# A second MoE call with rows cleared ahead, roots on ScalarE, and the pieces of attention's last eleven steps dealt out anew

## Chip, cores and metric

The kernel runs on one core of one Trainium2 chip. The metric is device time of the whole launch in microseconds, median of several executions.

## What is computed

Six residual updates on 2048 tokens of 128 channels (8 sequences of 256), in fp32. Cut to what matters here:

```python
x = x + 0.5 * moe(layernorm(x))          # first expert stage, f = 0
x = x + attention(layernorm(x))          # 16 heads of 8 channels
x = x + 0.5 * moe(layernorm(x))          # second expert stage, f = 1, same weights
x = x + 0.5 * channel_mix(layernorm(x))
x = x + gated_conv(layernorm(x))
x = x + 0.5 * channel_mix(layernorm(x))

def moe(s):
    h = rmsnorm(s @ W_in.T) * in_norm_w
    logits = h @ Wr.T
    idx = top2(logits + expert_bias)
    gates = softmax(logits[idx])                       # over the two
    out = sum over the two experts e of gates[e] * rmsnorm((silu(h @ Wg[e].T) * (h @ Wu[e].T)) @ Wd[e].T)
    return rmsnorm(out) @ W_out.T
```

`x` is not layer-normed on its own ahead of `W_in`: the kernel folds the mean into the weight and divides by one root of (mean square + scaled variance), called `ri` below.

## The kernel before

**Tokens.** `x` stays on the chip in four chunks of 512 tokens (four tiles of 128). PE, DVE, ACT and SP execute instructions in the order in which the code emits them; whatever is emitted first stands first in each engine's queue. GpSimd (POOL) keeps the order of the powers and scatters too.

**An expert stage** has three parts. `dispatch` (one call for each block of tokens: five blocks of 2 or 4 tiles, `LATE` being 4, 4, 4, 2, 2 for f = 1) has pieces: `turned` (transposes `pxt_f`, copied to `xnt_f`), `product` halves (`pin_f`, copied to `u_f`, squares summed into `ss_f`), `measured` (variance into `z_f`), `normed` (`ri_f`: for f = 0 a Sqrt on ACT and a reciprocal on DVE, for f = 1 a power on POOL), `logits` (`lg_f`), `scaled` (rows `hrow` on ACT), two `choices` (top 1 and top 2, six to eight small DVE operations each), `places` (ranks `prank_f` by matmuls, then `at_row`, `posi`: the row of each token in a table of rows sorted by expert), and `rows` (two indirect scatters for each tile, from POOL, into `hs` in DRAM).

`hs` has a region of 2304 rows of 129 floats for each of eight experts. `table` counts tokens for each expert and works out 24 turns (15 of 256 rows, 9 of 128). `zeros` writes 256 zero rows behind each expert's last row, four DMAs from SP and four from ACT, each with a start row from the count. `experts` then fetches for each turn the weights of its expert (`w_f`, 832 KB) and its rows (`hst_f`), three turns ahead, and runs gate (`pg_f`), up (`pu_f`), down (`py_f`) and a scatter of results into `y`. `combine` fetches `y`, weighs, norms, multiplies with `W_out` and adds to `x`.

**Attention** is a loop of 32 steps `s` (8 sequences times 4 groups of heads) and three to drain, each with halves a and b. TensorE makes the scores twice, once to find the largest (`pm`, DVE reduces it to `m`, transposed in `pmt`, added to the query rows as `qa`) and once transposed (`ps`), ACT takes the exponent (`es`), and two steps later `po` averages the values. `ps` has a single pair of banks, so `ps` of a half step waits until `es` of the one before has read it. Everything else is cut into pieces hung on a half step by `at(s, half, ...)`: the end of the first expert stage for chunks 1 to 3 (`combine`'s pieces), the norm and the query, key and value rows of each next chunk (`norm_sums` to `values`), the output of each sequence (`turn_back`, `turn_heads`, `out_heads`: `pot`, `rc`, `cc`, `pcc`, `ct`, `pwo`, added to `x`), and the pieces of the second dispatch (`leaving[0]` to `leaving[4]`). Most of these take their PSUM tile from one bank with the tag `sa`.

`to_heads` brings queries and keys into lanes of 32 partitions by a DRAM round trip: `heads` out, then four loads `qk` from SP. The first step to use chunk n's lanes is 8n.

The last sequence's output can be made only after step 31's average, that is after `osb` of half step (33, b). From there the code emits, in (34, a), the output of the last sequence, the end of block 3, and the whole of block 4. Then `table`, the gates and the experts follow.

## Time and profile before

| | |
|---|---|
| three runs | 680.30, 681.46, 682.06 us |
| profiled execution | 660.66 us in all, span 658.9, TensorE clock 0.92 |
| busy share | PE 79%, DVE 55%, ACT 42%, POOL 30% |
| first expert turns | about 66 to 185 us |
| attention's scores | from 204 us; `osb` of the last sequence at 396.87 us |
| second stage, first gate | 433.54 us; last down product ends about 546 us |
| tail | to 658.9 us |
| DMA | 69.80 MB; HBM written 14.38 MB |

Times of pieces are microseconds from the start of the span of the profiled execution. "Idle before <- X" names what ended an engine's idle time. In section 2 of the page a digit is the busy share of a slice of 16.5 us in tenths. The profiled execution is some 21 us shorter than the median of the runs, so a sum made on it is carried over as a difference.

### The profile page before, as it was taken

To read this page: it belongs to the slowest core of one execution; us is meant where nothing else is said; L and a number is where in the kernel's file an instruction comes from. 1 tells how busy PE (TensorE), PEld (TensorE's weight loads), DVE (VectorE), ACT (ScalarE), POOL (GpSimd) and SP (SyncE) were. 2 spreads that over 40 slices of the span, in tenths; PEclk is the share of its full clock that TensorE was granted. 3 is DMA by queue.
4 is the path that set the end of the run, shared out by engine and by line. 5 is a ranking of instruction groups with operands and counts; after the bars stand their busy time and mean duration, and the time that the engine had idled before them with its cause. 6 is when DMAs were issued, how large, how long until landed. Compare 5 with 4: busy or idle time off the path is not lost. (4 is left out here: it accounts for less than half of the span.)

```text
span 658.9 us, 11485 instructions
## 1 busy us (share of the span) xinstructions
PE 520.4 (79%) x3945; PEld 412.0 (63%) x3945; DVE 360.7 (55%) x1120; ACT 275.0 (42%) x677; POOL 197.9 (30%) x206
## 2 busy tenths in 40 slices
PE   4530999999948988898898984179989992579996
PEld 3530899999935545555554652169979991458885
DVE  4664346544433566765866664724434441667676
ACT  3450233223332465565654662113223230867355
POOL 0476067523331100102004516303333333521110
PEclk9999999999965899999999996579999997779999
DMA  6016577777521302021030101466776774100002
GB/s 212 33 48 171 183 210 242 213 226 216 171 81 32 65 34 33 1 52 14 1 66 22 37 10 41 105 219 197 234 212 205 217 219 115 31 0 2 1 1 64
DMA packets 39753, 69.80 MB, mean 106 GB/s; under 512 B 4939, under 2 KB 30066, under 8 KB 39568
## 3 DMA queue, kind: packets, MB, share of 16 engines
q1 hardware_dynamic: 34000, 59.55, 31.6%
q0 software_dynamic: 4544, 8.47, 3.8%
q10 hardware_dynamic: 1152, 1.06, 0.6%
q8 instruction: 31, 0.51, 0.3%
q14 instruction: 26, 0.21, 0.1%
HBM read 55.60 MB, written 14.38 MB: 106 GB/s over the span
## 5 line engine op out<-in xcount | busy, mean ns | idle before, releaser
L617 POOL DMA_INDIRECT y<-yrow_f,idx_f x78 | 76.6, 982 | 140.8 <-ACT sg_f L583 79.7
L955 ACT ACTIVATE es<-ps 128x1024 f32<-128x1024 f32 x64 | 65.4, 1022 | 59.0 <-PE ps L918 36.0
L428 POOL DMA_INDIRECT hs<-hrow,posi_f x64 | 62.0, 968 | 87.5 <-DVE ri_f L355 35.5
L938 DVE TENSOR_REDUCE m<-pm 128x4 f32<-128x1024 f32 x64 | 77.5, 1220 | 18.1 <-PE pm L901 18.1
L918 PE MATMUL ps<-qa,qk 32*128 32x256 f32 x512 | 75.4, 408 | 14.6 <-ACT es L955 10.3
L901 PE MATMUL pm<-qk 32*128 32x256 f32 x512 | 80.7, 419 | 5.1 <-DMA qk<-heads 3.7
L574 PE MATMUL pg_f<-ht_f,w_f 128*128 128x256 f32 (+1 forms) x384 | 79.6, 352 | 2.6 <-DVE idx_f L615 1.4
L597 PE MATMUL py_f<-w_f,hg_f 128*128 128x128 f32 x624 | 78.2, 276 | 2.6 <-DVE yrow_f L608 2.6
L597 PEld LDWEIGHTS py_f<-w_f,hg_f 128*128 128x128 f32 x624 | 75.2, 192 | 4.8 <-DVE yrow_f L608 3.4
L574 PE MATMUL pu_f<-ht_f,w_f 128*128 128x256 f32 (+1 forms) x384 | 76.5, 343 | 0.0
L590 DVE TENSOR_TENSOR hg_f<-pu_f,sg_f 128x1024 f32<-128x1024 f32 (+1 forms) x48 | 49.2, 1025 | 46.8 <-PE pu_f L574 46.7
L583 ACT ACTIVATE sg_f<-pg_f 128x1024 f32<-128x1024 f32 (+1 forms) x48 | 41.5, 864 | 67.1 <-PE pg_f L574 67.1
L574 PEld LDWEIGHTS pg_f<-ht_f,w_f 128*128 128x128 f32 x384 | 63.1, 197 | 9.1 <-DVE idx_f L615 1.6
L607 ACT ACTIVATE ysq_f<-py_f 128x128 f32<-128x128 f32 x78 | 21.1, 274 | 109.2 <-PE py_f L597 98.1
L574 PEld LDWEIGHTS pu_f<-ht_f,w_f 128*128 128x128 f32 x384 | 61.5, 193 | 6.0
L918 PEld LDWEIGHTS ps<-qa,qk 32*128 32x128 f32 x512 | 44.0, 187 | 31.8 <-ACT es L955 21.6
L901 PEld LDWEIGHTS pm<-qk 32*128 32x128 f32 x512 | 47.8, 193 | 10.2 <-DMA qk<-heads 6.2
L608 DVE TENSOR_TENSOR yrow_f<-py_f,w_f 128x256 f32<-128x256 f32 (+1 forms) x48 | 18.0, 375 | 52.1 <-ACT ysq_f L607 52.1
L566 DVE TENSOR_SCALAR ht_f<-pht_f,pack 128x256 f32<-128x256 f32 (+1 forms) x48 | 20.7, 432 | 41.8 <-PE pht_f L564 41.7
L564 PE MATMUL pht_f<-ident,hst_f 128*128 128x128 f32 x78 | 17.5, 290 | 31.6 <-DMA hst_f<-hs 31.6
L965 PE MATMUL po<-es,v 128*32 128x256 f32 x512 | 35.1, 393 | 0.0
L152 POOL TENSOR_TENSOR cf_f<-cf_f,mhalf 128x8 f32<-128x8 f32 (+1 forms) x9 | 13.5, 1504 | 67.4 <-DVE cf_f L673 65.9
(257 smaller groups left out, 822.8 us busy)
## 6 DMA issues: line engine op xcount, KB each, us to landing
w_f<-in_wall_dram SPq DMA_DIRECT2D x48, 832.0 KB
hst_f<-hs SPq DMA_DIRECT2D x30, 129.0 KB
y_f<-y SPq DMA_DIRECT2D x14, 258.0 KB
pack<-in_pack_dram SPq DMA_DIRECT2D x1, 1729.0 KB
heads<-qkc SPq DMA_DIRECT2D x3, 512.0 KB
qk<-heads SPq DMA_DIRECT2D x12, 128.0 KB
y<-yrow_f,idx_f POOLq DMA_INDIRECT x78, 5.0
hst_f<-hs SPq DMA_DIRECT2D x18, 64.5 KB
```

The costliest lines, as they stand in the source:

```text
L428: ins = nc.gpsimd.indirect_dma_start(out=hs, out_offset=bass.IndirectOffsetOnAxis(ap=st["posi"][:, t, k : k + 1], axis=0), in_=hrow[:, t, ...
L574: nc.tensor.matmul(ph[:, k, :], w[t][:, o + k * P : o + k * P + P], ht[t], start=True, stop=True)
L583: nc.scalar.activation(sg, pg, AF.Silu)
L590: nc.vector.tensor_mul(hg[t], pu, sg)
L597: nc.tensor.matmul(py[:, s, :], hg[t][:, k, ts(s, P)], w[t][:, 2 * DFF + k * D : 2 * DFF + k * D + D], start=(k == 0), stop=(k == NFC - 1),)
L607: nc.scalar.activation(sq[:, s], py[:, s], AF.Square, accum_out=yrow[:, s, D : D + 1])
L617: ins = nc.gpsimd.indirect_dma_start(out=y2, out_offset=bass.IndirectOffsetOnAxis(ap=idx[:, s : s + 1], axis=0), in_=yrow[:, s, :], in_off ...
L901: nc.tensor.matmul(sc[:, jj, i, :], qs[c][r, g, col + i * P : col + (i + 1) * P], ks[c][r, g, col : col + S], start=True, stop=True,)
L918: nc.tensor.matmul(sc[:, jj, i, :], ks[c][r, g, col + i * P : col + (i + 1) * P], tops[s][r, :], start=True, stop=True,)
L938: nc.vector.tensor_reduce(m, sc, AX.X, ALU.max, negate=True)
L955: nc.scalar.activation(es, sc, AF.Exp, scale=scale)
L965: nc.tensor.matmul(po[32 * j : 32 * j + 32, :], vs[c][:, (b % 2) * 2 + i, (g % 2) * (H // 2) + (g // 2) * 4 + j, :], ess[s, j // 2][:, j % ...
```

## The change

- There are two row tables in DRAM, one for each expert stage. The first is zeroed as before. For the second, `zeros` isn't called; `clear_rows` writes zeros over all its 18432 rows, in 12 DMAs of 1536 rows from ACT, hung on attention's half steps (s, b) for s = 2, 3, 4, 8 to 12 and 16 to 19. `first` is worked out for f = 0 only.
- The last two blocks of the second dispatch take `ri` as Sqrt on ACT and reciprocal on DVE. `root_table` (one Sqrt on a scalar tile, which loads the table of that function) is emitted in (33, b), ahead of `normed` of block 3. In the first stage the copy of the token numbers comes ahead of the root.
- For f = 1 the first three turns fetch rows ahead of weights, and the first turn's weights come in three DMAs: gate, up, and down with the norm weights.
- Query and key rows of chunks 1 to 3 are made half a step earlier each; for chunk 1 the norm is earlier too.
- The pieces of blocks 0 to 4 of the second dispatch are hung anew, most of all from step 20 to the end. In (34, a), block 3's choices and rows and block 4's pieces are dealt out between the pieces of the last sequence's output.

In the built program TensorE, DVE and POOL have the same work as before but for the powers (two fewer on POOL) and, on DVE, two reciprocals more and `first` once less; ACT has two roots, one scalar root, two table loads and 12 DMAs more and four DMAs fewer; SP has four zero DMAs fewer and two weight DMAs more.

```diff
-    hs = tc.dram_tile([HS_ROWS, ROW], F32, name="hs")
+    hss = [tc.dram_tile([HS_ROWS, ROW], F32, name=f"hs{f}") for f in range(2)]
...
             if f == 0:
+                nc.vector.tensor_copy(hrow[:, :, :, D].bitcast(I32), tokid[:, slots])
+            if f == 0 or i >= len(parts) - 2:
                 nc.scalar.activation(ri, ri, AF.Sqrt)
                 nc.vector.reciprocal(ri, ri)
-                nc.vector.tensor_copy(hrow[:, :, :, D].bitcast(I32), tokid[:, slots])
             else:
                 power_of(ri, ri, mhalf.to_broadcast([P, nt]))
...
-        first = t_([P, E], "first", I32)
-        nc.vector.tensor_tensor(first, pc, base, ALU.add)
-        zeros(f, first)
+        if f == 0:
+            first = t_([P, E], "first", I32)
+            nc.vector.tensor_tensor(first, pc, base, ALU.add)
+            zeros(first)
...
+    def clear_rows(i, n):
+        m = E * REGION // n
+        dst = hss[1][1 + i * m : 1 + (i + 1) * m, :].rearrange("(p r) w -> p r w", p=P)
+        nc.scalar.dma_start(dst, zero[:, 0:ROW].unsqueeze(1).to_broadcast([P, m // P, ROW]))
...
-            nc.sync.dma_start(w[t], a["wall"][bass.ds(e, 1), :, :].rearrange("o p f -> p (o f)"))
+            wall = a["wall"][bass.ds(e, 1), :, :].rearrange("o p f -> p (o f)")
+            ends = (0, DFF, 2 * DFF, WALL) if f and t == TURNS[0] else (0, WALL)
+            for o, end in zip(ends, ends[1:]):
+                nc.sync.dma_start(w[t][:, o:end], wall[:, o:end])
...
-            fetch_weights(t)
-            fetch_rows(t)
+            for fetch in (fetch_rows, fetch_weights) if f else (fetch_weights, fetch_rows):
+                fetch(t)
...
+                clears = [s for s in range(2, 20) if s % 8 < 5]
+                for i, s in enumerate(clears):
+                    at(s, "b", partial(clear_rows, i, len(clears)))
...
-                    at(o + 4, "b", partial(turn_rows, n))
-                    at(o + 5, "a", partial(to_heads, n, part=0))
-                    at(o + 5, "b", partial(to_heads, n, part=1))
+                        at(o + 4, "a", partial(turn_rows, n))
+                        at(o + 4, "b", partial(to_heads, n, part=0))
+                        at(o + 5, "a", partial(to_heads, n, part=1))
...
+                at(25, "b", logits, partial(scaled, [0, 1]))
+                at(26, "b", choices[0], partial(scaled, [2, 3]))
+                at(27, "b", choices[1])
+                at(28, "b", places)
...
-                at(31, "a", logits)
-                at(31, "b", scaled, choices[0])
-                at(32, "b", choices[1])
-                at(33, "a", places)
-                at(33, "b", rows)
+                at(30, "b", logits, partial(scaled, [0, 1]))
+                at(31, "a", partial(scaled, [2, 3]))
+                at(31, "b", choices[0])
+                at(32, "a", choices[1])
+                at(32, "b", places, rows)
...
-                at(32, "a", turned)
-                at(32, "b", half0, half1, measured, normed_)
-                at(33, "b", logits, scaled, choices[0])
+                at(32, "b", turned)
+                at(33, "a", half0, half1, measured)
+                at(33, "b", root_table, normed_)
                 at(
                     34,
                     "a",
                     partial(turn_back, B - 1),
-                    choices[1],
+                    logits,
+                    choices[0],
                     partial(turn_heads, B - 1),
+                    scaled,
                     partial(out_heads, B - 1),
                     t2,
                     measured2,
+                    choices[1],
+                    h20,
+                    h21,
                     places,
-                    h20,
                     rows,
-                    h21,
                     normed2,
```

## The prediction

> **What bounds the kernel now.** First the slices of the page: TensorE is at 9 tenths or more through both expert stages and attention, and falls to 4 tenths at 395 to 412 us and to 1 at 412 to 428 us. So I read the hand-over from attention to the second expert stage; from the chain of waits:
>
> ```profile
> 422.13 0.96 POOL hs L428
> 423.09 0.30 issue
> 423.39 6.37 DMA hs<-hrow,posi_f
> ...
> 429.96 2.21 DMA hst_f<-hs
> 432.17 0.14 issue
> 432.30 0.67 PE pht_f L564 x2
> ...
> 433.54 3.78 PE pg_f L574 x8
> ```
>
> The last scattered row block takes 6.37 us to land; the first row fetch waits for it. The tile view of `hs` gives the usual time:
>
> ```profile
> DMA to landing us min/median/max: 2.3/2.3/6.4
> ```
>
> The timeline of the same stretch shows what runs ahead of the scatter and beside it:
>
> ```profile
> 396.87 0.59 ACT L974 COPY osb<-po 128x512 f32<-128x512 f32 x1 [1.23 <-PE po L965]
> ...
> 398.20 0.36 DVE L869 RECIPROCAL rc<-pot 128x32 f32<-128x32 f32 x1
> ...
> 404.25 1.27 PE L341 MATMUL pin_f<-win_r,xnt_f 128*128 128x136 f32 x4 [0.27 <-DVE at_row_f L418]
> ...
> 411.50 0.96 POOL L428 DMA_INDIRECT hs<-hrow,posi_f  x1 [0.30 <-issue]
> 412.48 0.72 POOL L152 TENSOR_TENSOR ri_f<-ri_f,mhalf 128x2 f32<-128x2 f32 x1
> 413.24 0.17 DVE L366 TENSOR_TENSOR lg_f<-u_f,ri_f 128x16 f32<-128x16 f32 x1 [6.37 <-POOL ri_f L152]
> ...
> 419.97 4.06 ACTq L522 DMA_DIRECT2D hs<-zero  x4
> 420.25 4.28 SPq L522 DMA_DIRECT2D hs<-zero  x4
> ```
>
> The root of the last block's norm is a POOL power; it is queued behind twelve scatters, so VectorE stands 6.37 us. Then eight zero writes of 129 KB share the DMA engines with the last four scatters. Last, attention, from the waits between 185 and 436 us:
>
> ```profile
> PE ps L918 <- ACT es L955: 10.3, 21, 1.0
> ...
> PE pm L901 <- DMA qk<-heads: 3.7, 4, 1.5
> ```
>
> and from its timeline:
>
> ```profile
> 302.25 0.48 PE L901 MATMUL pm<-qk 32*128 32x256 f32 x1 [1.51 <-DMA qk<-heads]
> ...
> 358.73 0.48 PE L918 MATMUL ps<-qa,qk 32*128 32x256 f32 x2 [1.93 <-DVE qa L950]
> ```
>
> A step lasts some 5.2 us and TensorE is busy nearly all of it, so only such waits can go; work that is reordered there is worth nothing by itself.
>
> [...] the four last scatters land after 3.2, 3.8, 4.9 and 6.4 us as zero writes from two other queues pile up. [...] the trace shows 1.28 for each load, at 427.45 for one[...].
>
> **The change, part by part.** Times are of the profiled execution (span 658.9, 660.66 us in all); its start of a part minus the new one is the gain.
>
> *Attention, to_heads half a step earlier.* The last pieces of the key and query loads arrive late at steps 8, 16 and 24: by about 1.3 us at 258.0, 1.9 at 302.3, 0.6 at 343.3 and 1.4 at 347.3, with smaller breaks before (weight loads stand 6.2 us for them, matmuls 3.7). Half a step is 2.6 us and covers each. I take -4.5; bounds -2.5 (clears in front of the transfer at step 13) and -5.5.
>
> *Choice of chunk 1 a step later.* At 356.48 VectorE starts eight small operations before `qa`, which began only at 358.16; TensorE stood 1.93. Now `qa` is next after `lg_f`, at about 356.7. I take -1.3; bounds -1.9 and 0, as the eight operations (1.7 us) go before the next step's `qa`.
>
> *Twelve clears on ScalarE's queue.* Each writes 792 KB from 1536 runs of 516 bytes; none stands in the trace. Bounds by the nearest rows: the issue of 128 runs takes 0.33 us, of 256 0.38, of 512 0.38 to 0.51, so 1536 is estimated at 0.8; the longest issue anywhere is 1.81, the eighth of a burst of `y_f` loads. ScalarE usually stands 1.0 to 1.6 us ahead of an `es`, so in half steps without other work the issue is free; about seven of twelve have copies or norms as well. All hidden is 0, none hidden 12 x 0.8 = 9.7; I take +2.0. The data themselves: 516-byte packets take 28 ns, 96 per engine is 2.7 us plus 2.3, under the 5.2 us of a step. At step 3 norm rows (1.65 us on ScalarE) now share a half step with value copies and a clear: +0.7, bounds 0 and 1.5. Attention: -4.5 - 1.3 + 2.0 + 0.7 = -3.1.
>
> *End of attention.* `pxt_f_3` now stands behind `prank_f_2` and ahead of the last `ps` on TensorE, and both use the one bank `sa`: it waits until VectorE has read the ranks. `po` of step 32 ends at 392.84, six rank matmuls take 1.3 (as at 394.50 to 395.80), `at_row` 0.2, the two transposes 0.4: the last `ps` starts at 394.85 for 393.44. `u_f_3` and its squares (1.1) now come ahead of `osb` on ScalarE, which ends its copy near 398.8 for 397.46: +1.4; bounds +0.7 and +2.
>
> *The last chain, from the end of `osb`.* Before: `rc` 0.74 later, `lg_f_4` 15.8 later. After, ScalarE loads the root table (1.28), warms it and takes the root of block 3 (0.4), VectorE's reciprocal (0.2) stands ahead of `rc`: `rc` comes 1.9 after `osb`, 1.2 of that new. `cc`, `pcc`, `ct`, `pwo` 2.7, as before; `x` follows after eight choice operations that fit beside these, 0.4; transposes 0.7 and copy 0.4; `pin` at once, no more behind the ranks, 1.3. The ranks of block 3 wait for the copy of `u_f` (same bank; 0.4, its squares run beside the ranks): they take 1.5, then `at_row` to `posi` 0.9, and only then VectorE reaches `ri_f_4`; root on ScalarE and reciprocal 0.7. `lg_f_4` is 11.1 after `osb`: 11.1 - 15.8 = -4.7. [...] From `lg_f` to `posi` stays 5.5 (413.24 to 418.74), and POOL is free by then, as block 2's scatters start earlier.
>
> *The landing.* Before, the first fetch goes out at 429.96, 11.2 after `posi`. After: POOL starts 0.78 after `posi`, its fourth scatter 3.87 later, and lands in 2.3: 6.95. The table is ready as late (its last write is at 424.82, 6.1 after `posi`, and drops 0.3 without `first`; load and registers 1.0: 6.8), so the landing decides, 7.0: -4.2; bounds -3.5 and -4.5. SP loses four zero writes, covered by that figure.
>
> *Rows ahead of weights.* The first weights used to go out at 425.60, hidden by the wait. Now they follow the first row fetch by 1.2 us, in three pieces. A 256 KB piece is estimated from the 832 KB one at 431.15, which landed 4.5 later[...]. Gate can start 4.1 after the fetch; before, it started 3.58 after. +0.5. The next weights leave 3.1 later than they would and land about 8.8 after the fetch, while gate and up take until 10: no new wait. Bounds 0 and +2.5.
>
> *With one answer:* the table loads for Exp and Silu lie in ScalarE's free time (it stands 13 us before `gates`); the token copy ahead of the reciprocal in the first stage is 0.2 us at most; the separate `hs` takes no wait away, since the first stage's fetches are long done.
>
> Sum: -3.1 + 1.4 - 4.7 - 4.2 + 0.5 = -10.1. The span becomes 648.8, the execution 650.6. The timed runs have a median of 681.46, 20.8 above that execution; nothing shows in which stage, so the gain is carried over as it is: 671.4.
>
> **Rivals.** *A, attention gives it back.* The 10.3 us that TensorE already waits for `es` speak for it: clears hidden at no half step (+9.7 for +2.0) leave -2.4, or 679.1. If half is hidden, +4.9 and -7.2: 674.2. Against it: ScalarE is only about half busy there. *B, slower: clears hold ScalarE's queue.* If an issue lasts as long as its runs take to be handed out, every `es` behind it is late, and with a single bank pair for `ps` TensorE stands as long. Idle 1.3 covers the start; each us above it costs 12. It decides from 12 x (t - 1.3) = 12.1, where t is 2.3 us; at 3.0 the clears cost 20 in place of 2, so +8: 689. For it: the 1.81 us issue, after some 3500 runs; against it, a clear has 1536 and 5 us until the next. *C, more.* If weights are in time, the clears are free and the end of attention comes no later, it is -10.1 - 0.5 - 2.0 - 1.4 = -14.0, or 667.5, and with the other bounds -17: 664.5. *D.* The zero writes might not be what delays the landing; then -5.9: 675.6. The rows' spread (2.3 to 6.4) speaks against it.
>
> **How the numbers follow.** The forecast, 667 to 675: 0.58. A and D, 675 to 680: 0.20. C, below 667: 0.10. B, above 681: 0.12. About 0.3% (2 us) is what a measurement tells from none. The range leaves out half of C and most of B: 665 to 680. Slower by over 0.3% is most of B, 0.11; within it a little of A and B, 0.05; faster 0.84.
>
> **What would show it.** In the new profile: scatters near 2.3 us to landing, no zero writes at the table, row fetch some 12 us earlier (near 418), gate near 422; waits on `qk<-heads` gone; clear issues under 1 us and `es` waits little over 10; `rc` about 1.9 after `osb`. Clears over 2 us, or `es` waits above 20, make me wrong.

## The result, and the profile after

| | median of runs | runs | ratio to before, 95% interval |
|---|---|---|---|
| before, first comparison | 680.88 us | 4 | |
| changed, first comparison | 671.85 us | 4 | 0.9883 [0.9843, 0.9922] |
| before, second comparison | 657.92 us | 24 | |
| changed, second comparison | 652.76 us | 6 | 0.9928 [0.9894, 0.9962] |

The changed kernel is faster by 9.0 us in the first comparison and by 5.2 us in a second one; the forecast was 671.4 us, 10.1 less than before. The time was hit; several terms of the sum behind it were not.

One thing has to be cleared away first. The profile before spans 658.9 us and its runs take 681; the profile after spans 672.0 and was one of the runs of the table. The chain of waits of the profile after has pieces that the one before lacks (start, length, what ended it):

```profile
38.71 4.67 another core or an unknown queue
60.38 2.43 another core or an unknown queue
65.20 1.84 another core or an unknown queue
366.34 6.08 another core or an unknown queue
389.60 4.48 another core or an unknown queue
394.69 2.32 another core or an unknown queue
```

They make 21.8 us: an engine stands although, by the records, the work that it waits for has ended, and the profile names nothing else. Without them the span would be 650.2, where the sum said 648.8. Experiments 1 to 8, the changed kernel's among them, have none: they belong to the occasion on which a kernel ran and not to the change. So I read stages from two profiles free of them, experiment 1 (before) and experiment 5 (changed), and use the profile after only where no pause falls.

The end of attention and the last chain of the profile after, in its timeline:

```profile
418.08 0.58 ACT L990 COPY osb<-po 128x512 f32<-128x512 f32 x1 [0.16 <-issue]
...
420.39 0.34 DVE L885 RECIPROCAL rc<-pot 128x32 f32<-128x32 f32 x1
...
429.95 0.17 DVE L371 TENSOR_TENSOR lg_f<-u_f,ri_f 128x16 f32<-128x16 f32 x1
...
435.38 0.17 DVE L428 CAST posi_f<-pos_f 128x4 int32<-128x4 f32 x1 [0.22 <-issue]
```

```profile
442.88 0.39 SPq L574 DMA_DIRECT2D hst_f<-hs  x1
444.09 1.41 SPq L568 DMA_DIRECT2D w_f<-in_wall_dram  x3
...
446.82 3.75 PE L590 MATMUL pg_f<-ht_f,w_f 128*128 128x256 f32 x8 [0.90 <-DMA w_f<-in_wall_dram]
447.62 0.34 SPq L568 DMA_DIRECT2D w_f<-in_wall_dram  x1
...
453.81 1.53 PE L590 MATMUL pg_f<-ht_f,w_f 128*128 128x256 f32 x6 [0.93 <-DMA w_f<-in_wall_dram]
```

The reader is to see four distances. From the end of `osb` (418.66) to `rc` 1.7 us (0.74 before), to the last `lg_f` 11.3 (15.8 before), from the end of `posi` (435.55) to the first row fetch 7.3 (11.2 before), from there to the first gate 3.9 (3.6 before). All four are near the forecast. The last line is a wait that was not foreseen: the second gate stands 0.93 us for its weights.

The waits of attention in the same profile (engine, line waited for: us in total, times, longest):

```profile
PEld pm L917 <- DMA qk<-heads: 3.1, 3, 1.4
...
PE pm L917 <- DMA qk<-heads: 1.8, 2, 1.0
```

Before it was 6.2 and 3.7. These waits were to be gone; they are only halved.

### The profile page after: what moved, and what is told of

It reads as the page before. It is cut to its first block, busy times and chain, and to the rows that moved or that the text cites. A ratio compares the mean times of both kernels' runs of the same rounds, so it can differ in the third digit from the quotient of the medians.

```text
span 672.0 us, 11456 instructions
## 1 busy us (share of the span) xinstructions
PE 526.8 (78%) x3945; PEld 415.8 (62%) x3945; DVE 361.6 (54%) x1121; ACT 277.6 (41%) x682; POOL 196.0 (29%) x204
## 4 chain that ended last, share of the span: by engine, by line
PE 60%; DVE 11%; ACT 9%; DMA 9%; issue 4%; another core or an unknown queue 3%; SPq 1%; POOL 1%; ACTq 0%; DVEq 0%; POOLq 0%
PE pg_f L590 10%; PE py_f L613 10%; PE pu_f L590 9%; PE ps L934 7%; PE po L981 3%; ACT es L971 3%; DMA qk<-heads 3%; PE pvf L1291 2%; PE pgo L1318 2%; DMA y<-yrow_f,idx_f 2%; PE pm L917 2%; DMA w_f<-in_wall_dram 2%; PE pk_m L1235 1%; PE pht_f L580 1%
## 5 line engine op out<-in xcount | busy, mean ns | idle before, releaser
L981 PE MATMUL po<-es,v 128*32 128x256 f32 x512 | 36.6, 401 | 0.0
L966 DVE TENSOR_TENSOR qa<-pmt,qk 128x256 f32<-128x256 f32 x32 | 13.5, 422 | 38.4 <-PE pmt L960 28.9
```

The costliest lines, as they stand in the source:

```text
L981: nc.tensor.matmul(po[32 * j : 32 * j + 32, :], vs[c][:, (b % 2) * 2 + i, (g % 2) * (H // 2) + (g // 2) * 4 + j, :], ess[s, j // 2][:, j % ...
```

## The experiments

All are edits of the changed kernel unless told otherwise. "Time" is the median; the kernel before took 657.7 us (30 runs) beside experiments 1 to 4, 657.92 (24) beside 5 to 8, 680.45 (11) beside 9 to 11 and 678.06 (11) beside 12.

### 1. The kernel before, once more

No edit.

> The kernel before, unchanged, profiled once more. Its first profile spans 658.9 us while its timed runs take 679 to 682; the changed kernel's profile spans 672.0 and holds about 21.8 us of stretches in which nothing that the trace shows is waited for. Theory pauses: they belong to the execution and not to the kernel; this profile then spans 675 to 682 and shows such stretches of 15 to 25 us in all, and with them taken out the stages last as in the first profile. Rival: the change brought them; then this profile spans 657 to 662 again without any.

661.06 us, span 659.3, and no such pause. That is what the rival had named, but this profile alone doesn't decide: beside experiments 1 to 4 the kernel before takes 657.7 us in 30 runs, on an occasion without pauses. What decides is that the changed kernel's profiles of that time (experiments 2 to 8) have none either, while all five taken where the kernel before took 678 to 681 have them (the profile after and experiments 9 to 12), at the same places of the program whatever the edit: in those of experiments 9 and 11, 4.7 us at 38 us and 6.1, 4.5 and 2.3 us in the last steps of attention. No profile of the kernel before holds them; that it had them too rests on its runs, which are 23 us longer there. What the engines wait for is open.

### 2. The fetches in the old order

```
-        for fetch in (fetch_rows, fetch_weights) if f else (fetch_weights, fetch_rows):
-            fetch(t)
+        fetch_weights(t)
+        fetch_rows(t)
...
-    ends = (0, DFF, 2 * DFF, WALL) if f and t == TURNS[0] else (0, WALL)
+    ends = (0, WALL)
```

> The changed kernel, with the second expert stage's first three fetches as before (weights ahead of rows, the first weights in one piece). Theory: the rows wait for the scatters' landing and the table is ready only some 1.2 us before that, so weights first gain little for the first gate (0 to 0.5 us later after the landing), but the second weights leave some 2 us earlier and the 0.9 us wait of the second gate goes: 0.5 us faster than the changed kernel in all, 0 to 1. Rival (the order was worth its place): an 832 KB load takes 4.5 us to land, and beside the last scatters longer, so the first gate comes 1 us or more later than 3.94 us after the row fetch, and the kernel is 1 to 2 us slower.

653.19 us, ratio 0.993 [0.9897, 0.9964]: no difference from the changed kernel (0.9928) that these runs can tell. In its profile the first row fetch comes 3.78 us after the last scatter's start (2.67 in experiment 5), the first gate 5.86 after the fetch (4.14), and the time from turn 0's Silu to turn 1's is 4.64 (5.38). From `posi` to turn 1's Silu the old order is 2.1 us longer. In this stage the rival is right: now that rows land early, the old order no longer hides the first weights. In the runs the difference does not show.

### 3. Roots on GpSimd again

```
-            if f == 0 or i >= len(parts) - 2:
+            if f == 0:
...
-                at(33, "b", root_table, normed_)
+                at(33, "b", normed_)
```

> The changed kernel, with the roots of the last two blocks' norms taken by GpSimd's power again, and no root table loaded there. Theory: the power of block 3 stands behind the eight scatters of block 2 (415.7 to 425.6), so its logits come about 5 us later than 421.1, and that of block 4 stands behind the four scatters of block 3, some 10 us later than 429.95; less the 1.2 us of table load ahead of the last heads' reciprocal: 8 us slower than the changed kernel, 6 to 10. Rival: the chain was long for another reason (reads, ranks, transposes), and the root's place counts only for the 4.7 us by which the last chain became shorter: 3 to 5 us slower.

662.32 us, ratio 1.0076 [1.005, 1.0101], 9.6 us above the changed kernel's 652.8: the theory's size, not the rival's. Its timeline shows both powers behind scatters:

```profile
404.65 0.72 POOL L156 TENSOR_TENSOR ri_f<-ri_f,mhalf 128x2 f32<-128x2 f32 x1
405.41 0.17 DVE L371 TENSOR_TENSOR lg_f<-u_f,ri_f 128x16 f32<-128x16 f32 x1 [3.56 <-POOL ri_f L156]
...
418.28 0.72 POOL L156 TENSOR_TENSOR ri_f<-ri_f,mhalf 128x2 f32<-128x2 f32 x1
...
419.04 0.17 DVE L371 TENSOR_TENSOR lg_f<-u_f,ri_f 128x16 f32<-128x16 f32 x1 [6.32 <-POOL ri_f L156]
```

VectorE stands 3.56 and 6.32 us. From the end of `osb` to the last `lg_f` it takes 19.2 us, for 11.3.

### 4. Every clear issued twice

```
-                    at(s, "b", partial(clear_rows, i, len(clears)))
+                    at(s, "b", *[partial(clear_rows, i, len(clears))] * 2)
```

> The changed kernel, with each of the twelve clears issued twice. A clear's 1536 packets of 516 bytes take some 5 us on the DMA engines in the trace, so two fill more than a step. Theory transfer: what a clear costs is that the heads' round trip to memory stands behind its packets (the first such write took 4.75 us to land where 2.6 is usual); doubled, the heads of steps 5 and 13 come 4 to 6 us later each and the waits on qk<-heads grow from 1.8 to about 10 us: 6 to 10 us slower than the changed kernel. Theory issue: a clear costs ScalarE's time alone (0.54 us each, mostly hidden): 12 x 0.54 = 6.5 us more of issue, mostly hidden, 0 to 3 us slower, the qk waits unchanged and the es waits up.

746.75 us, ratio 1.1332 [1.1278, 1.1385]: outside both. The two clears write the same rows, so ScalarE waited for the first to land before it issued the second (in ten of twelve cases; the waits of `es` on `hs<-zero` alone are 41.1 us, up to 9.1 each, and those of all instructions 95.9, for 94.0 lost). The run measured a wait that the edit had added, and says nothing on either theory. Experiment 10 repairs it.

### 5. The changed kernel, once more

No edit.

> The changed kernel once more, on the chip on which the kernel before takes 657.7 us and shows none of the stretches without a cause. My sum says -10.1 us: ratio 0.985. By the variant with the old fetch order (654.6 us span; attention to the end of the last osb copy 195.5 us against 193.6 before, the last row fetch to the second gate's end some 2.7 us longer than in the changed kernel's own profile) it takes 650.5 us, ratio 0.989: attention gives back 3.6 us of what I had counted. If the gain were what the first comparison showed only because of the stretches without a cause, the ratio would be 0.993 or nearer to 1.

652.76 us, ratio 0.9928 [0.9894, 0.9962], span 652.0, no pauses. The stages, in us, from the two profiles without pauses:

| stage | before (1) | changed (5) | difference |
|---|---|---|---|
| first `pm` to step 3's first `m` | 26.1 | 24.3 | -1.8 |
| to the last `m` | 156.8 | 153.3 | -3.5 |
| to the end of the last `osb` | 10.7 | 16.0 | +5.3 |
| to the last `lg_f` | 15.8 | 11.3 | -4.5 |
| to the end of `posi` | 5.5 | 5.6 | +0.1 |
| to the first row fetch | 11.5 | 7.3 | -4.2 |
| to turn 1's Silu | 11.3 | 13.3 | +2.0 |
| to the end | 217.2 | 216.7 | -0.5 |

The first line is no gain of the change: it is 26 to 27 us in experiments 1, 2, 3, 6, 7 and 8, and in experiment 5 TensorE happened to be granted its full clock at 212.6 us, in the others between 217 and 220. The last line varies too: it is 213.8 in experiment 7 and 214.6 in experiment 2. So 2 us in either of these two lines say nothing. Without the first line the profiles differ by 5.5 us, close to what the runs say (5.2). Attention gave nothing: what its steps won went in its last 16 us. Its steps one by one, from the start of each step's first `m` (us; six of the profiles without pauses):

```
steps        3-6    7-8   15-16  23-24  25-27  28-30
before (1)  19.85  12.72  13.14  14.19  16.70  15.05
2           19.79  11.38  12.65  11.65  14.16  15.57
3           19.79  11.77  13.35  11.66  14.16  15.58
5           19.79  11.72  14.63  11.65  14.16  15.58
6           19.79  12.87  12.59  11.65  14.16  15.25
8           19.79  10.08  10.92  11.66  14.15  15.60
```

Experiments 2, 3, 5 and 6 leave these steps as the change made them, up to step 29. The steps left out, up to step 30, differ by less than half a microsecond each way.

### 6. Block 2's logits and scaled rows at their old places

```
-                at(30, "b", logits, partial(scaled, [0, 1]))
-                at(31, "a", partial(scaled, [2, 3]))
-                at(31, "b", choices[0])
+                at(31, "a", logits)
+                at(31, "b", scaled, choices[0])
```

> The changed kernel, with the logits and the scaled rows of block 2 at their places of before (a half step and a whole step later). Theory root: in the changed kernel ScalarE stands 2.4 us at 379.8 in front of block 2's scaled rows, since their root is a GpSimd power queued behind chunk 1's scatters; the next es is late by as much, TensorE stands 2.1 us, and the granted clock falls to half in the stretches that follow, so that the ranks, the last ps and the last po take up to twice their time (last max to the end of osb 20.1 us against 12.2 before). With the rows later the stall goes, TensorE keeps its clock until the last osb, and the kernel is 4 to 7 us faster than the changed one. Rival: the clock falls because the last steps are thin on matmuls whatever comes before; then only the 2 us stall goes, or nothing, 0 to 2 us faster, and the ranks of block 2 still take over 3 us.

649.48 us, ratio 0.9894 [0.9843, 0.9944]. By the runs it is 3.3 us below the changed kernel, where 4 to 7 were expected, and the intervals don't separate the two; the profiles show what happened. The changed kernel (experiment 5), timeline:

```profile
377.67 1.04 POOL L156 TENSOR_TENSOR ri_f<-ri_f,mhalf 128x4 f32<-128x4 f32 x1
378.75 0.91 ACT L376 ACTIVATE hrow<-u_f,ri_f 128x256 f32<-128x256 f32 x2 [2.44 <-POOL ri_f L156]
379.56 1.00 ACT L971 ACTIVATE es<-ps 128x1024 f32<-128x1024 f32 x1
380.62 0.48 PE L934 MATMUL ps<-qa,qk 32*128 32x256 f32 x2 [2.12 <-ACT es L971]
...
389.29 1.43 PE L406 MATMUL prank_f<-mask_f,ones 128*128 128x24 f32 x6
392.09 2.08 PE L934 MATMUL ps<-qa,qk 32*128 32x256 f32 x8
```

and its windows (stretch: length, busy time of each engine with instructions, granted clock, DMA share, GB/s):

```profile
387.00:397.00 10.00, 9.71 (x57) 5.90 (x56) 2.37 (x14) 3.50 (x8) 3.18 (x4) 0.50 0.05 18
```

Experiment 6, the same places:

```profile
387.43 0.81 PE L406 MATMUL prank_f<-mask_f,ones 128*128 128x24 f32 x6
...
389.13 1.13 PE L934 MATMUL ps<-qa,qk 32*128 32x256 f32 x8
```

```profile
386.00:390.00 4.00, 3.72 (x39) 2.49 (x36) 2.30 (x13) 1.40 (x2) 0.00 (x0) 1.00 0.00 0
```

Read the first fence from the top. The power of block 2 stands behind chunk 1's scatters and ends at 378.71. ScalarE, which meets the scaled rows ahead of the next `es`, stands 2.44 us for it, TensorE 2.12 for that `es`. Some 6 us later its clock is granted at 0.50 for 10 us, and the six rank matmuls take 1.43 us for 0.81, the last eight `ps` 2.08 for 1.13. In experiment 6 there is no such stall, the clock stays at 1.00, and from the last `m` to the end of `osb` it takes 12.0 us, for 16.0. Steps 28 to 30 are 0.3 us shorter and step 31 1.3 (from its first `m` to its second 1.41 us, for 2.67): 5.6 us in all in this pair of profiles. The five profiles without pauses that have the changed order of these pieces (2, 3, 5, 7, 8) have 15.7 to 17.4 us in that last stretch, and the clock at 0.50 within it. In the three stretches of 3.4 us ahead of the fall (376.4 to 386.6 us) TensorE was busy 62%, 76% and 72%, at the full clock. Stretches at 0.50 last 3.4 us in the profile before (359.5 to 362.9), 6.8 and 10.2 in the profile after (372.7 to 379.5, 393.2 to 403.4). What a fall goes by, and whether the stall leads to the one 6 us later, is not settled here.

### 7. The heads half a step later, as before

```
-                        at(o + 4, "a", partial(turn_rows, n))
-                        at(o + 4, "b", partial(to_heads, n, part=0))
-                        at(o + 5, "a", partial(to_heads, n, part=1))
+                        at(o + 4, "b", partial(turn_rows, n))
+                        at(o + 5, "a", partial(to_heads, n, part=0))
+                        at(o + 5, "b", partial(to_heads, n, part=1))
```

(and the same for chunk 1.)

> The changed kernel, with the turning of the rows and the projections to the heads at their old half steps. My term: half a step covers the late key and query loads, 4.5 us: that much slower than the changed kernel. Theory clears: the clears ahead of the heads' round trip lengthen it by about 2 us where they overlap, so half a step gained only some 2.5 us in all; and without it the waits on qk<-heads are 7 to 9 us rather than the 5 of before, and the kernel is 3 to 6 us slower. Rival: the half step moved other work against TensorE and gained nothing: 0 to 1 us slower.

658.56 us, ratio 1.0019 [0.9988, 1.005], 5.8 us above the changed kernel: in the range that theory clears gave, but not where it said. The steps that need the loads (7, 8, 15, 16, 23, 24) take 36.8 us together, for 38.0 in experiment 5 and 36.9 as the mean of 2, 3, 5 and 6, and the waits on `qk<-heads` are those of experiment 5 (3.7 and 2.2 us, for 3.6 and 2.2). What is longer is steps 13 and 14, 21 and 22 (11.76 us each pair, for 9.96) and 3 to 6 (21.74 for 19.79). In the two pairs the timeline has a wait of its own:

```profile
290.52 0.59 ACT L842 COPY qkc<-pqk 128x512 f32<-128x512 f32 x1 [0.44 <-PE pqk L841]
291.13 0.33 SPq L846 DMA_DIRECT2D heads<-qkc  x1
291.16 0.66 PE L323 MATMUL pxt_f<-ident,x 128*128 128x128 f32 x4 [0.68 <-ACT qkc L842]
```

The change also moved the transposes of chunks 0 and 1's dispatch to (13, b) and (21, b), and both pieces use the bank `sa`: put back alone, the heads collide with them. In steps 3 to 6 it is another wait:

```profile
236.69 0.48 PE L934 MATMUL ps<-qa,qk 32*128 32x256 f32 x2 [2.22 <-ACT es L971]
```

In the changed kernel the transposes of the norm rows (`pxn_a`, 1.48 us) fill most of that gap; put back, they leave it open, and TensorE's clock is at 0.50 from 237.1 to 240.5. The edit undoes one part against another and does not measure the half step. What it shows beside that: at steps 23 and 24, which have no clears ahead, the old place costs 1.2 us (12.88 for 11.66), and at 15 and 16, which have, it costs nothing (11.50 for 12.6 to 14.6). And the write of the heads, issued at 291.13 after the clear has drained, lands 2.76 us later (the loads leave at 293.89).

### 8. Zero writes at the table, no clears

```
-        if f == 0:
-            first = t_([P, E], "first", I32)
-            nc.vector.tensor_tensor(first, pc, base, ALU.add)
-            zeros(first)
+        first = t_([P, E], "first", I32)
+        nc.vector.tensor_tensor(first, pc, base, ALU.add)
+        zeros(f, first)
...
-                for i, s in enumerate(clears):
-                    at(s, "b", partial(clear_rows, i, len(clears)))
```

> The changed kernel, without the twelve clears and with the eight zero writes of the second stage at the table, as before. My term: the zero writes delay the landing of the last scatters, so the first row fetch comes 10.5 to 11.5 us after posi in place of 7.3; the clears cost attention 2 us: 2 us slower than the changed kernel, 0.5 to 3.5. Theory clears: their packets delay the heads' round trip; without them the waits on qk<-heads fall from about 1.8 to 0 and attention is 1.5 to 2.5 us shorter. Rival D: the zeros are not what delays the landing: then the fetch stays at 7 to 8 us and the kernel is 1 to 2 us faster.

653.09 us, ratio 0.9922 [0.9894, 0.995]: no difference from the changed kernel, and two effects against each other. From `posi` to the first row fetch 10.0 us, for 7.3 (my term, a little smaller; rival D, 7 to 8, falls). And steps 7, 8, 15, 16, 23 and 24 take 32.7 us, for 36.9 (mean of 2, 3, 5 and 6; 35.7 to 38.0): the clears cost attention 4.2, all of it in steps 7, 8, 15 and 16, which have clears ahead of their loads. Before, the same steps took 40.05: without clears the half step is worth 7.4, with whatever else the change moved in these steps. The waits on `qk<-heads` fall from 3.6 us (weight loads) to one of 0.3. How the clears do it shows in SyncE's DMA issues, the write of the heads and the loads that wait for it to land. Before (experiment 1), at step 13:

```profile
288.44 0.33 SPq L830 DMA_DIRECT2D heads<-qkc  x1
291.19 2.89 SPq L833 DMA_DIRECT2D qk<-heads  x4
```

The changed kernel (experiment 5), and experiment 8:

```profile
282.74 0.33 SPq L846 DMA_DIRECT2D heads<-qkc  x1
288.37 2.94 SPq L849 DMA_DIRECT2D qk<-heads  x4
```

```profile
284.02 0.33 SPq L845 DMA_DIRECT2D heads<-qkc  x1
287.71 2.89 SPq L848 DMA_DIRECT2D qk<-heads  x4
```

The write of the heads takes 2.75 us, 5.63 beside the clears, and 3.69 without them. At step 5 the same three distances are 2.69, 4.88 and 2.68, so the 0.9 us left at step 13 without clears is not theirs. With experiment 7's 2.76 this says: half a step earlier is half a step deeper into the clears.

One more thing comes out of experiments 1, 2, 5 and 8 together. From the end of `posi` to turn 1's Silu it takes 22.8 us before, 22.8 without zero writes but with the old order of fetches (2), 22.8 with the new order but with zero writes (8), and 20.6 with both changed (5). Each part alone moves the first row fetch and brings nothing at turn 1; only the two together bring 2.2 us. These are single profiles, and the runs don't resolve it; the other seven profiles that have both changed and this order of fetches take 19.7 to 21.3.

### 9. Five repairs at once

Experiment 6's edit; block 3's `turned` moved from (32, b) to (32, a), so that its transposes no longer stand behind block 2's ranks; its `normed` after `turn_back`; clears from runs of two rows (as in experiment 11); and another order of fetches:

```
-                at(32, "a", choices[1])
+                at(32, "a", leaving[3][0], choices[1])
...
-                at(32, "b", turned)
...
-                at(33, "b", root_table, normed_)
+                at(33, "b", root_table)
...
                     partial(turn_back, B - 1),
+                    normed_,
                     logits,
...
-        for t in TURNS[:3]:
-            for fetch in (fetch_rows, fetch_weights) if f else (fetch_weights, fetch_rows):
+        for i, t in enumerate(TURNS[:3]):
+            for fetch in (fetch_rows, fetch_weights) if f and i == 0 else (fetch_weights, fetch_rows):
```

> The changed kernel with five repairs: block 2's logits and scaled rows at their places of before; block 3's transposes a half step earlier, so that the last ps stands no more behind the reading of block 2's ranks; block 3's root after the last heads' reciprocal; the second weights ahead of the second rows; and each clear from runs of two rows (1032 bytes, half as many packets). From the traces: -3.4 (clock kept to the last osb), -0.7, -1.0, -1.2 (the second gate's wait), -2.0 (two of the three waits on qk<-heads): 8.3 us below the changed kernel's 652.8, 644.5 us, ratio 0.980 to the kernel before, 0.975 to 0.986. If the granted clock falls at the end of attention for another reason, 648 to 650, ratio 0.985 to 0.988.

671.41 us beside 680.45: ratio 0.9881 [0.9833, 0.9929], missed. One repair was a harm, in the timeline:

```profile
439.12 3.75 PE L590 MATMUL pg_f<-ht_f,w_f 128*128 128x256 f32 x8 [1.02 <-DMA w_f<-in_wall_dram]
439.91 0.38 SPq L574 DMA_DIRECT2D hst_f<-hs  x1
...
445.87 0.66 PE L580 MATMUL pht_f<-ident,hst_f 128*128 128x128 f32 x2 [3.00 <-DMA hst_f<-hs]
446.33 3.62 PE L590 MATMUL pu_f<-ht_f,w_f 128*128 128x256 f32 x8
```

The second rows, issued at 439.91 behind 832 KB of weights, land 6 us later, and their transpose stands ahead of the first `pu_f`: Silu to Silu 9.84 us, for 5.2 to 5.4.

### 10. Twelve more clears, to memory of their own

```
+    hss = [tc.dram_tile([HS_ROWS, ROW], F32, name=f"hs{f}") for f in range(3)]
...
-                    at(s, "b", partial(clear_rows, i, len(clears)))
+                    at(s, "b", partial(clear_rows, i, len(clears)), partial(clear_rows, i, len(clears), 2))
```

> The changed kernel, with twelve more clears at the same half steps, to memory of their own that nothing reads, so that no clear waits for another of the same rows. Theory transfer: a clear's 1536 packets take about 5 us on the DMA engines; two in one step leave no gap, the heads' round trips at steps 5 and 13 stand behind a backlog and the waits on qk<-heads grow from about 2 to 8 to 14 us: 6 to 12 us slower than the changed kernel. Theory issue: twelve more issues of 0.54 us on ScalarE, mostly in its free time: 0 to 3 us slower, the waits on qk<-heads unchanged.

732.93 us beside 680.45, ratio 1.0773 [1.0709, 1.0837]: some 60 us above the changed kernel, and both theories missed it. The tile view of `zero`, of the changed kernel (experiment 5) and of this one (duration of one issue, min/median/max, in ns):

```profile
L539 ACTq DMA_DIRECT2D hs<-zero x12: 541/542/654, 222.4 to 318.7; - x12
```

```profile
L539 ACTq DMA_DIRECT2D hs<-zero x24: 546/2310/6064, 232.7 to 381.4; - x24
```

An issue that lasted 0.54 us now lasts 2.3 in the middle and up to 6.1. Summed over the instructions, ScalarE's queue is held 64.7 us by 24 issues, for 6.6 by 12: 58 us more, close to the whole loss. The waits on `qk<-heads` grew by only 5 us on the matmuls. So what the prediction's rival B named, issues that hold ScalarE's queue, does happen at twice the rate of clears; what such an issue waits for is not shown here.

### 11. Clears from runs of two rows

```
-        dst = hss[1][1 + i * m : 1 + (i + 1) * m, :].rearrange("(p r) w -> p r w", p=P)
-        nc.scalar.dma_start(dst, zero[:, 0:ROW].unsqueeze(1).to_broadcast([P, m // P, ROW]))
+        dst = hss[1][1 + i * m : 1 + (i + 1) * m, :].rearrange("(p r k) w -> p r (k w)", p=P, k=2)
+        nc.scalar.dma_start(dst, zero[:, 0 : 2 * ROW].unsqueeze(1).to_broadcast([P, m // P // 2, 2 * ROW]))
```

> The changed kernel, with each clear written from runs of two rows: 768 packets of 1032 bytes for 1536 of 516. Theory transfer: a packet takes 47 ns for 28, so the packets of a clear take some 40% less of the DMA engines, the first heads' write lands in about 2.7 us again for 4.75, and the waits on qk<-heads mostly go: 1 to 2.5 us faster than the changed kernel. Theory issue: the issue of half the runs costs ScalarE 0.5 us for 0.54: no difference.

670.51 us beside 680.45, ratio 0.9856 [0.9797, 0.9914]; the changed kernel has 0.9883 beside 680.88, so by the runs the 1.8 us are not separated from nothing. The page shows the mechanism (packets, MB, share of 16 engines), first of experiment 5, then of 11:

```profile
q10 hardware_dynamic: 19200, 10.04, 10.4%
```

```profile
q10 hardware_dynamic: 9984, 10.04, 5.2%
```

Without clears the queue has 0.6% (experiments 1 and 8). A clear thus takes 9.8% of 652 us by 12, 5.3 us on all 16 engines; from runs of two rows 4.6% of 668.2 by 12, 2.6 us. The bytes are the same and the packets half as many: on the mean each takes about 55 ns in either form. Steps 7, 8, 15 and 16, where no pause falls, take 21.4 us, for 24.6 in the profile after and 21.0 without clears (experiment 8): the clears are free now in these steps. (Steps 3 to 6 take 21.4, for 19.8 in the profile after. There the clock is at 0.50 from 245.0 to 248.4, behind no wait of TensorE over 0.7 us; experiment 12 has the same, 9 has not.) The waits on `qk<-heads` fall to 0.8 (weight loads) and 0.4 us (matmuls), from 3.1 and 1.8.

### 12. The repairs without the harmful one

Experiment 9, with the rows of each turn ahead of its weights again, and the last third of turn 0's weights behind turn 1's:

```
+        later = None
         for t in TURNS[:3]:
-            for fetch in (fetch_rows, fetch_weights) if f else (fetch_weights, fetch_rows):
-                fetch(t)
+            if f:
+                fetch_rows(t)
+                rest = fetch_weights(t)
+                if later:
+                    later()
+                later = rest
+            else:
+                fetch_weights(t)
+                fetch_rows(t)
```

> The five repairs of the last combination but one: block 2's logits and scaled rows at their old places, block 3's transposes a half step earlier, block 3's root after the last reciprocal, clears from runs of two rows; for the fetches, the rows of every turn stay ahead of the next weights, and only the last third of the first turn's weights (which its down projection needs some 10 us later) goes behind the second turn's weights. The earlier combination lost 4.4 us between the first two gates, where the second rows landed 6 us after their issue behind 832 KB of weights. Without that: sg of turn 0 to turn 1 4.0 to 5.0 us in place of 9.84 (5.4 in the changed kernel), and the whole 5 us below the earlier combination: ratio to the kernel before 0.975 to 0.984, taken 0.980. If the repairs of attention were worth less than the traces say, 0.985 to 0.988, no better than the changed kernel.

667.27 us beside 678.06, ratio 0.9819 [0.9787, 0.985]. That is inside the range expected and the best ratio of all, below the kernel before and by its median below the changed one; against the changed kernel's 0.9883 [0.9843, 0.9922] the intervals just overlap. The second gate no longer waits:

```profile
442.38 3.38 PE L596 MATMUL pg_f<-ht_f,w_f 128*128 128x256 f32 x8 [0.99 <-DMA w_f<-in_wall_dram]
...
447.54 1.89 PE L596 MATMUL pg_f<-ht_f,w_f 128*128 128x256 f32 x8
```

Silu to Silu is 3.67 us, for 5.2, and `rc` comes 0.75 us after `osb`, for 1.7. Steps 7, 8, 15 and 16 take 21.1 us. What the repairs of attention's end brought here can't be read, since pauses fall there.

## Why the prediction was right, and where it was not

The time was right; the sum behind it had five terms wrong, partly against each other.

| term of the sum | predicted | measured | by |
|---|---|---|---|
| heads half a step earlier | -4.5 | -7.4 | steps 7, 8, 15, 16, 23, 24, 8 against 1 |
| twelve clears | +2.0 | +4.2 | the same steps, 2, 3, 5, 6 against 8 |
| choice of chunk 1 a step later | -1.3 | -2.5 | steps 25 to 27, 5 against 1 |
| norm rows of step 3 | +0.7 | -0.1 | steps 3 to 6, 5 against 1 |
| end of attention, ranks ahead of the last `ps` | +1.4 | +1.3 | last `m` to `osb`, 6 against 1 |
| block 2's rows earlier | not in the sum | +5.6 | 5 against 6 |
| last chain | -4.7 | -4.5 | 5 against 1 |
| landing | -4.2 | -4.2 | 5 against 1 |
| rows ahead of weights | +0.5 | +2.0 | first row fetch to turn 1's Silu, 5 against 1 |
| sum | -10.1 | -5.6 | |

The two profiles differ by 5.5 us without their first line. Not every row is isolated by a run: the heads and the choice of chunk 1 above all are read from stages in which other pieces moved too.

**The last chain** holds in mechanism and size, and experiment 3 confirms the root from the other side.

**The landing** holds in size, but only in part by its mechanism. Of the 4.2 us the zero writes are 2.7 (8 against 5). And in experiment 5 the landing no longer decides: the chain of waits runs from `posi` through the table to the fetch,

```profile
420.62 0.18 DVE tab_tab L507
...
422.02 0.39 SPq L574
```

The table is written 6.1 us after `posi`, and the fetch goes out 1.2 later. The last scatter is issued 4.7 us after `posi`, and the others of its kind land in 2.3 to 2.5, so it is there at about 7.1, just before. The prediction had the table at 6.8 and the landing at 7.0 and called the landing; the two stand close, the other way round. The other 1.5 us of the 4.2 (8 against 1) go with the order of the fetches, to which the landing's term gave nothing: in experiment 2, with the old order and no zero writes, the rows go out 8.4 us after `posi`, 1.4 behind the weights in SyncE's queue.

**The missing step is block 2's.** The prediction read the power queued behind scatters for the last block, and did not ask the same of block 2, whose logits and scaled rows the diff moves half a step and a whole step earlier, in front of an `es` on ScalarE. It is not in the sum at all. The stall itself is 2.1 us; the rest goes with TensorE's clock (0.50 from 387 to 397 us in experiment 5, 1.00 from 376 to 394 in experiment 6), for which the sum had no term: its durations came from a profile in which the clock was full from 219.6 us until after `osb`, but for one stretch (359.5 to 362.9).

**The choice of chunk 1** shows the same two things, a wait and a fall of the clock behind it, on the other side: the move is worth 2.5 us, not 1.3, and more than the whole wait of 1.9. No run moves this choice alone. Before (experiment 1), in the timeline and in the windows:

```profile
359.24 0.48 PE L918 MATMUL ps<-qa,qk 32*128 32x256 f32 x2 [1.94 <-DVE qa L950]
```

```profile
353.00:360.00 7.00, 4.96 (x68) 3.28 (x70) 5.98 (x20) 2.63 (x3) 4.32 (x5) 1.00 0.06 20
360.00:363.40 3.40, 3.40 (x30) 1.23 (x26) 3.13 (x8) 1.26 (x2) 2.63 (x3) 0.50 0.20 63
```

After the wait the clock is at 0.50 for one stretch of 3.4 us.

**Heads and clears** were -2.5 us together and are -3.2, but by other sizes on both sides. The clears were priced by ScalarE's issue (0.8 us each, partly hidden). An issue takes 0.54 and is hidden (steps 9 to 12 take 21.6 us with clears and without; the waits of `ps` on `es` are 11.9 us, for 10.3, so rival A's mechanism is not what gave attention's gain back); the cost comes by the clears' packets on the DMA engines: with half as many the waits on `qk<-heads` fall from 3.1 and 1.8 us to 0.8 and 0.4 (experiment 11). I had seen that path and dismissed it: 2.7 us of packets at 28 ns each plus 2.3, under a step of 5.2. The packets take 5.3 us, twice the estimate, so a clear fills a step and the heads' write stands beside it. The 28 ns is a median, and the sum of many packets goes by their mean: where nothing else moves data (the clears issued at 300.8 and 308.8 us of experiment 5) the median is 28 ns too, but the mean is 45, and in other clears up to 68. Hence the waits on `qk<-heads` that were to vanish and did not, at steps 8 and 16; at step 24, with no clears ahead, they went. The lower bound of the heads' term (-2.5, clears in front of the transfer) had named this and was put aside. The prediction had read the same of the scatters, which landed after 3.2 to 6.4 us beside zero writes from two other queues; here, at step 5 the heads' round trip took 4.88 us beside the clears and 2.68 without.

**Rows ahead of weights.** The first gate came as forecast, 3.9 to 4.1 us after the fetch. The forecast's time for a 256 KB piece was my estimate; in the profile after, the gate starts 2.7 us after the issue of its weights began (444.09 to 446.82). "No new wait" was wrong: the second weights, issued 4.7 us after the fetch, land 6.1 us later beside the first weights, not 4.1 as I had them (8.8 less 4.7). The second gate waited 0.9 us. But the +2.0 is no price of the order: experiment 2 puts the old order back and is 2.1 us later at turn 1's Silu. The landing and this term are one stage, cut at a fetch that itself moved; together they are -2.2, where -3.7 was forecast, and neither part of the change brings them alone (experiments 2 and 8). The prediction's own signs didn't fit its sum either: a row fetch near 418 and a gate near 422 are 12 us earlier, while its terms up to the fetch make 10.6 and up to the gate 10.1.

**The carrying over.** The prediction took the gain over to runs 20.8 us longer as it was. With the pauses the gain was 9.0, without them 5.2. Experiment 5's expectation had named a ratio of 0.993 as the sign that the first gain rests on the pauses, and 0.9928 came; but the intervals overlap, so that the pauses make the gain larger is not shown. What can be read is where they hide a loss. In the profile after, ScalarE waits 1.2 us for block 2's root (2.44 in experiment 5), the clock has fallen behind the pause at 366 us (0.50 from 372.7) and is full again from 379.5, and the ranks take

```profile
384.16 0.81 PE L406 MATMUL prank_f<-mask_f,ones 128*128 128x24 f32 x6
```

as in experiment 6; from the last `m` to the end of `osb` it is 12.0 us there, as in experiment 6, and not 16.0. So the largest loss that the sum left out is mostly absent from the comparison that the forecast was made for. That the forecast came within half a microsecond is luck in good part: its misses ran against each other, and this one did not show.

## What to carry to other kernels

Two stalls of TensorE in a dense loop went with more than their own length here, each with a stretch at half clock behind it (3.4 and 10 us): where a wait of 1.9 us went, the steps became 2.5 shorter, and one of 2.1 went with 5.6 in one pair of profiles (3.3 by the medians of the runs). When the clock falls can't be told ahead from these runs. When a piece moves earlier in one engine's queue, look up what its operands wait for on the other engines at the new place, for every block and not only the last one. Price a background write by its packets at their mean time (a clear took 5.3 us, where the median had given 2.7), and look at the round trips beside it (the heads' took 4.88 us, for 2.68); halving the packets took nearly all of its cost in the steps read here (24.6 us to 21.4, for 21.0 without it). And when two parts of a change feed one fetch, try each alone and both: here neither alone brought anything at the second turn.

## What the hardware showed that I had not expected

- Packets of 516 and of 1032 bytes took about the same on the mean in such a write: 5.3 us for 1536 of them, 2.6 us for 768, on 16 engines, about 55 ns each. Their medians differ (36 and 47 ns).
- With two writes of 1536 packets in a half step, a DMA issue on ScalarE held its queue for up to 6.1 us (2.3 in the median of experiment 10's 24), where one write in a half step took 0.54 (experiment 5).
- The granted clock of TensorE fell to half behind a stretch in which it was busy 72% of the time (changed kernel, experiment 5, 383.2 to 386.6 us), and stayed full behind one of 62% (376.4 to 379.8). In experiment 11 it fell behind one of 74% (241.6 to 245.0), with no wait of TensorE over 0.7 us ahead of it (each stretch lasts 3.4 us). A bound isn't to be had from these runs.
- The kernel before took 657.9 us in one comparison and 680 in another; where it took 680, the changed kernel's profile has six pauses of 1.8 to 6.1 us, and they come at fixed places of the program in the five profiles of such times. Their cause is open.
